# A graph attention layer whose neighbour sums go partly through TensorE: scaled rows summed by transposes, one more column of A, and an earlier flag

## The chip, the cores and the metric

The kernel runs on one core of one Trainium2 chip. The metric is the device time of one execution in microseconds. A core has TensorE (PE; its weight loads are shown as PEld), VectorE (DVE), ScalarE (ACT), GpSimd (POOL) and SyncE (SP), each of which works through its own instructions in a fixed order, and 16 DMA engines that the queues share.

## The reference

There are 3327 nodes with 1024 features; `adj` is symmetric with the diagonal set, about 17 neighbours a row. `bf`, `bg` and `bW` are zero in the data, but the kernel handles them as they come.

```python
h = jnp.maximum(_layernorm(x, axis=-1), 0.0)
f = h @ Wf + bf
g = h @ Wg + bg
e = jax.nn.relu(f @ g.T)
scores = jnp.where(adj > 0, e, NEG)
attention = jax.nn.softmax(scores, axis=1)
x_W = h @ W + bW
return x + attention @ x_W
```

## The kernel before, in words

The scores are needed only where there is an edge, so the kernel (`edge_path`) gathers neighbours. It uses f . g = h (Wf Wg^T) h'^T + terms of the biases, and sums the neighbours' h before it multiplies by W.

Phase 1 (to about 300 us) writes the normalised rows h to memory (`hd`) and each row's list of neighbours (`pd`), ranks the rows by degree into 26 tiles of 128 (`perm`; tile 25 has 127 rows), and makes A = Wf Wg^T (`make_A`, L512), the column u = Wf bg (`uT`, L525 to L528), the row v = bf Wg^T and the number c = bf bg (`make_rows`, L530). v and bW are kept as three bf16 parts each (`split3`, L345, a chain of ten small VectorE operations) and added to a product by a matmul with a matrix of ones over three partitions.

Phase 2 goes over the tiles. A tile has a fixed number of neighbour slots, its cap:

```python
CAPS = [37, 25, 23, 22, 21, 21, 20, 20, 19, 19, 18, 18, 17, 17, 17, 16, 16, 15, 15, 15, 14, 14, 13, 13, 12, 11]
```

For a tile s there are these steps.

- `prepare(s)` (L637): gathers the lists (`pi`) and the tile's own rows (`hp`), transposes hp on TensorE (L632) with copies by ACT (L633) into hT, and makes q = hT' A in two blocks of 512 columns (L650, with the bias row L651, copied by ACT in L652). Eight one-column matmuls (L655) make h.u, to which ACT adds c (`ci`, L657). `df` is the degree column, compared with the cap into `bads` (L659, L660).
- `dots`: for each slot POOL gathers 128 rows of h into a buffer G (L621, a pool of 23 buffers), and VectorE multiplies by q and sums over the row, starting at ci (L673, output `junk`, the sum in `sc`).
- `softmax` (L678) over the tile's scores; its last part on VectorE is the reciprocal `rs` (L696) and the scaling by it (L699). Tiles of cap over 20 (0, 1, 2, 3, 4, 5) go in two halves, the second of which rescales.
- `combine` (L710) forms y, the weighted sum of the gathered rows. Slot 0 starts y on ACT (L732). Most slots are added on VectorE (L734, one pass over 128 x 1024 each). Some, in the tile's last half alone, go to TensorE: ACT writes a diagonal matrix of the weights (L723), and eight fp32 matmuls with it, one for each 128 columns, accumulate the slot's rows, transposed, in the PSUM tile `yT_ps` (L727; an fp32 matmul is two instructions in the trace, so 16 a slot). `on_tensor` (L704) says how many: (4 cap - 52) // 5, which is 16, 9, 8, 7, 6, 6, 5, 5, 4, 4, 4, 4, 3, 3, 3, 2, 2, 1, 1, 1 for tiles 0 to 19 and 0 after, 94 in all.
- `project(s)` (L736): gathers the rows of x (`xp`), adds y's own transposition into the same PSUM tile by eight matmuls with the identity (L746), or transposes y as hp if the tile has no slot there; ACT copies (L751); 16 matmuls by W in two halves, with bW (L756, L757), end in `ps_o`, a ring of two.
- `finish(s)` (L760): VectorE adds x (L765), POOL scatters the rows to `out` (L766).

The program issues dots of tile s + 1 among the steps of tile s, and `prepare(s + 2)` behind `project(s)`. The order on each engine is not written out by hand: a scheduler moves instructions by its own estimate, keeping the dependences, and G's 23 buffers decide when a load can start. At the end VectorE takes the maximum over `bads` (L807), a one-by-one matmul brings it to one partition (L811), VectorE casts it to `flag` (L812), and every engine loads it (L823) and branches (L824): above zero a dense path would compute everything again. That path doesn't run with these data.

## Time and profile before

| what | us |
|---|---|
| runs | 1549.21, 1552.29, 1556.26 (median 1552.29) |
| the profiled execution | 1548.85 |
| its span | 1547.1 |
| PE busy | 1282.8 (83%) |
| DVE busy | 1314.7 (85%) |
| ACT busy | 350.9 (23%) |
| POOL busy | 920.8 (60%) |

The span is what the profile covers; the profiled execution's own time is 1.75 us longer. A row of a timeline reads: start, duration, engine, line, operation, output <- inputs, shapes, count, and in brackets the idle time of the engine before it and what ended it. A row of the waits reads: who waited for what, us in total, times, the longest. PEclk is the clock that TensorE was granted, 1 being full speed. A group of PE rows overlaps its neighbours a little, since matmuls are pipelined.

### The profile page before, as it was taken

The numbers are of one execution on the slowest core, as the hardware profiler recorded it, in microseconds if no ns is written. First come the engines' busy times: TensorE is split into PE (matmuls) and PEld (weight loads), VectorE is DVE, ScalarE is ACT, GpSimd is POOL, SyncE is SP. The second block draws the span as 40 slices with busy tenths as digits, with TensorE's granted clock in tenths as the row PEclk, the third lists the DMA queues.
The fourth block names the chain that finished last, engine by engine and source line by source line (L and its number), as shares of the span: only waits on it lengthen the run. The fifth ranks groups of instructions, "written<-read, shape, count | busy, mean of one in ns | idle before, by whom it ended". The sixth has DMA issues, their size and how long they took to land.

```text
span 1547.1 us, 15226 instructions
## 1 busy us (share of the span) xinstructions
PE 1282.8 (83%) x4904; PEld 718.8 (46%) x4904; DVE 1314.7 (85%) x2664; ACT 350.9 (23%) x646; POOL 920.8 (60%) x625
## 2 busy tenths in 40 slices
PE   1259899394799999999999999999999866979922
PEld 1125453242556765575656545555555432434410
DVE  5878878969799999999998989999999998598750
ACT  6666666110211211121111111111111100011100
POOL 7667867166567665646656566667675666344510
PEclk9999899597899999999999989999999877989966
DMA  8788876387688877858866678777786778445510
GB/s 337 278 349 305 315 265 207 96 349 271 208 318 301 277 250 262 309 177 291 299 241 222 234 245 285 260 264 265 259 283 227 242 250 265 149 146 159 118 41 16
DMA packets 124451, 372.67 MB, mean 241 GB/s; under 512 B 41025, under 2 KB 41425, under 8 KB 121033
## 3 DMA queue, kind: packets, MB, share of 16 engines
q0 software_dynamic: 106288, 286.92, 54.9%
q1 hardware_dynamic: 10860, 70.49, 12.5%
q10 hardware_dynamic: 7212, 14.18, 2.5%
q8 instruction: 41, 0.67, 0.2%
q14 instruction: 50, 0.41, 0.1%
HBM read 343.63 MB, written 27.80 MB: 240 GB/s over the span
## 4 chain that ended last, share of the span: by engine, by line
PE 50%; issue 12%; DVE 8%; POOL 5%; DMA 3%; ACT 1%; POOLq 0%; ACTq 0%; DVEq 0%
PE ps_o L756 19%; PE ps_q L650 15%; PE yT_ps L727 8%; DVE y L734 5%; POOL G L621 4%; PE yT_ps L746 2%; PE ps_t L655 2%; DVE junk L673 2%; DMA G<-hd,pi 2%; PE ps_t L632 1%; PE ps_o L757 1%; PE ps_q L651 1%; DMA xp<-in_x_dram,perm 1%; DVE xp L765 0%; ACT hT L633 0%
## 5 line engine op out<-in xcount | busy, mean ns | idle before, releaser
L621 POOL DMA_INDIRECT G<-hd,pi x468 | 599.2, 1280 | 313.9 <-DVE y L734 128.1
L673 DVE CUSTOM_DVE_ANT_0 junk<-G,q,ci 128x1024 bf16<-128x1024 f32 (+1 forms) x468 | 600.1, 1282 | 49.1 <-DMA G<-hd,pi 37.8
L734 DVE SCALAR_TENSOR_TENSOR y<-G,sc,y 128x1024 f32<-128x1024 f32 (+1 forms) x348 | 447.2, 1285 | 14.6 <-ACT y L732 9.4
L650 PE MATMUL ps_q<-A_sb,hT 128*128 128x512 f32 (+1 forms) x832 | 384.1, 612 | 29.3 <-ACT q L652 24.2
L756 PE MATMUL ps_o<-W_sb,yT 128*128 128x512 f32 (+1 forms) x832 | 383.1, 615 | 4.1 <-ACT yT L751 2.9
L650 PEld LDWEIGHTS ps_q<-A_sb,hT 128*128 128x128 f32 (+1 forms) x832 | 156.2, 195 | 210.5 <-issue 177.7
L756 PEld LDWEIGHTS ps_o<-W_sb,yT 128*128 128x128 f32 (+1 forms) x832 | 159.5, 196 | 202.1 <-issue 189.0
L443 POOL TENSOR_TENSOR r<-r,iotaj 128x3327 f32<-128x3327 f32 (+1 forms) x26 | 188.3, 7250 | 74.4 <-ACT r L442 62.9
L727 PE MATMUL yT_ps<-diag,G 128*128 128x128 f32 x1504 | 176.0, 279 | 1.4 <-ACT diag L723 1.4
L727 PEld LDWEIGHTS yT_ps<-diag,G 128*128 128x128 f32 x1504 | 172.9, 195 | 7.0 <-ACT diag L723 3.6
L452 DVE MAX8 cand<-r 128x8 f32<-128x208 f32 (+2 forms) x416 | 134.0, 361 | 36.7 <-POOL r L443 36.6
L521 PE MATMUL ps_A<-WgT,WfT 128*128 128x512 f32 x256 | 120.6, 631 | 2.9 <-ACT WfT L493 2.9
L652 ACT COPY q<-ps_q 128x512 f32<-128x512 f32 (+1 forms) x52 | 29.4, 591 | 295.4 <-PE ps_q L651 203.9
L521 PEld LDWEIGHTS ps_A<-WgT,WfT 128*128 128x128 f32 x256 | 50.8, 202 | 75.1 <-issue 64.8
L633 ACT COPY hT<-ps_t 128x512 f32<-128x512 f32 (+1 forms) x52 | 29.3, 590 | 220.8 <-PE ps_t L632 128.3
L442 ACT ACTIVATE r<-a 128x3327 f32<-128x3327 int32 (+1 forms) x26 | 77.1, 2967 | 7.8 <-issue 7.8
L765 DVE TENSOR_TENSOR xp<-ps_o,xp 128x512 f32<-128x512 f32 (+1 forms) x52 | 35.7, 687 | 43.6 <-PE ps_o L757 43.6
L766 POOL DMA_INDIRECT out_dram<-xp,perm x26 | 37.8, 1452 | 57.3 <-DVE flag L812 28.2
L621 POOL DMA_INDIRECT xp<-in_x_dram,perm x26 | 29.6, 1137 | 69.3 <-DMA out_dram<-xp,perm 64.1
L621 POOL DMA_INDIRECT hp<-hd,perm x26 | 28.3, 1089 | 63.0 <-PE ps_t L632 36.1
L746 PE MATMUL yT_ps<-ident,y 128*128 128x128 f32 x320 | 48.4, 315 | 20.1 <-DVE y L734 20.1
L746 PEld LDWEIGHTS yT_ps<-ident,y 128*128 128x128 f32 x320 | 46.1, 228 | 23.5 <-DVE y L734 21.8
(139 smaller groups left out, 892.6 us busy)
## 6 DMA issues: line engine op xcount, KB each, us to landing
a<-in_adj_dram SPq DMA_DIRECT2D x25, 1663.5 KB, 8.9
xt<-in_x_dram SPq DMA_DIRECT2D x25, 512.0 KB, 4.3
hd<-xt ACTq DMA_DIRECT2D x25, 512.0 KB, 5.9
G<-hd,pi POOLq DMA_INDIRECT x468, 6.0
wr<-in_L_gnn_Wg_dram SPq DMA_DIRECT2D x8, 512.0 KB, 6.1
wr<-in_L_gnn_Wf_dram SPq DMA_DIRECT2D x8, 512.0 KB, 5.0
W_sb<-in_L_gnn_W_dram SPq DMA_DIRECT2D x1, 4096.0 KB, 14.7
a<-in_adj_dram SPq DMA_DIRECT2D x1, 1455.6 KB, 10.4
```

Source lines behind the costliest of these rows:

```text
L442: nc.scalar.activation(r[:n], a[:n], AF.Relu, accum_out=deg[:n, t : t + 1])
L443: nc.gpsimd.tensor_mul(r[:n], r[:n], iotaj[:n])
L452: nc.vector.max(cand[:n, s * 8 : s * 8 + 8], r[:n, s * SW : min(N, (s + 1) * SW)])
L521: nc.tensor.matmul(ps, WfT[:, k, :], WgT[:, k, o * CB : (o + 1) * CB], start=(k == 0), stop=(k == KD - 1))
L621: nc.gpsimd.indirect_dma_start(out=to, out_offset=None, in_=table, in_offset=bass.IndirectOffsetOnAxis(ap=idx, axis=0),)
L650: nc.tensor.matmul(ps[:n], hT[:, k, :n], A_sb[:, k, o * CB : (o + 1) * CB], start=(k == 0), stop=False)
L673: nc.vector.tensor_tensor_reduce(junk[:n], g[:n], e["q"][:n], 1.0, e["ci"][:n], op0=ALU.mult, op1=ALU.add, accum_out=e["sc"][:n, k : k + 1],)
L727: nc.tensor.matmul(e["yT"][:, c, :n], g[:n, c * P : (c + 1) * P], diag[:n, :n], start=(k == pe[0] and c % 4 == 0), stop=False, skip_group_ ...
L734: nc.vector.scalar_tensor_tensor(y, g[:n], p, y, op0=ALU.mult, op1=ALU.add)
L746: nc.tensor.matmul(e["yT"][:, c, :n], e["y"][:n, c * P : (c + 1) * P], ident[:n, :n], start=False, stop=(c % 4 == 3), skip_group_check=True,)
L756: nc.tensor.matmul(ps[:n], yT[:, k, :n], W_sb[:, k, o * CB : (o + 1) * CB], start=(k == 0), stop=False)
L766: ins = nc.gpsimd.indirect_dma_start(out=out[:, :], out_offset=bass.IndirectOffsetOnAxis(ap=perm[:n, s : s + 1], axis=0), in_=e["xp"][:n], ...
```

## The change

**The slots on TensorE.** `on_tensor` gives cap - 13 slots for (4 cap - 52) // 5: 16, 10, 9, 9, 8, 8, 7, 7, 6, 6, 5, 5, 4, 4, 4, 3, 3, 2, 2, 2, 1, 1 for tiles 0 to 21 and 0 after, 122 in all for 94. A slot is now scaled by ACT in place (the whole G, 128 x 1024, after's L728) and then transposed onto `yT_ps` by eight transposes with the identity that accumulate (after's L711, function `sum_transposed`); the diagonal and its pool are gone. y is added by the same function. VectorE's additions of a slot to y fall from 348 to 320.

**h.u as a column of A.** `A_sb` and `v3` get a column 1024 for u and c, and two of zeros, 1026 in all, so that q is made in three blocks of 342. The one-column matmuls and `ci` are gone; the dot starts at column 1024 of q. c goes through a split3 of its own in `make_rows`.

**The flag.** It is computed in `failed()`, called behind `prepare(25)`, which the program issues in tile 23's turn, and loaded there in the program.

```diff
@@ -296,12 +296,15 @@
...
     O = W.shape[1]
     P = 128
     CB = 512
     KD = D // P
+    QB = 342
+    QW = 3 * QB
     NT = (N + P - 1) // P
     OH = O // CB
     SW = -(-N // SEG)
@@ -336,10 +339,10 @@
     nc.gpsimd.memset(bads, 0.0)
 
     perm = const.tile([P, NT], I32, name="perm")
-    A_sb = wts.tile([P, KD, D], FP, name="A_sb")
-    uT = wts.tile([P, KD], FP, name="uT")
-    c_sb = wts.tile([P, 1], FP, name="c_sb")
-    v3 = wts.tile([3, D], BF, name="v3")
+    A_sb = wts.tile([P, KD, QW], FP, name="A_sb")
+    v3 = wts.tile([3, QW], BF, name="v3")
+    nc.gpsimd.memset(A_sb[:, :, D:], 0.0)
+    nc.gpsimd.memset(v3[:, D:], 0.0)
     bW3 = wts.tile([3, O], BF, name="bW3")
 
     def split3(pool, to, of):
@@ -495,13 +498,11 @@
         WgT = c1.tile([P, KD, D], FP, name="WgT")
         bfT = c1.tile([P, KD], FP, name="bfT")
         bgT = c1.tile([P, KD], FP, name="bgT")
-        bgr = c1.tile([P, KD, P], FP, name="bgr")
         bf3 = c1.tile([P, KD, 3], FP, name="bf3")
         bWf = c1.tile([3, O], FP, name="bWf")
         nc.gpsimd.dma_start(bfT, bf.rearrange("(k p) -> p k", p=P))
         nc.gpsimd.dma_start(bgT, bg.rearrange("(k p) -> p k", p=P))
         nc.gpsimd.dma_start(bWf, bass.AP(tensor=bW.tensor, offset=bW.offset, ap=[[0, 3], [1, O]]))
-        nc.vector.tensor_copy(bgr, bgT[:, :, None].to_broadcast([P, KD, P]))
         nc.vector.tensor_copy(bf3, bfT[:, :, None].to_broadcast([P, KD, 3]))
 
         def load_Wg(c):
@@ -525,14 +526,14 @@
             ps = p_u.tile([P, P], FP, name="ps_u")
             for k in range(KD):
                 nc.tensor.matmul(ps[:, 0:1], WfT[:, k, :], bgT[:, k : k + 1], start=(k == 0), stop=(k == KD - 1))
-            nc.scalar.copy(uT[:, c : c + 1], ps[:, 0:1])
+            nc.scalar.copy(A_sb[:, c, D : D + 1], ps[:, 0:1])
 
         def make_rows():
 
             ps = p_u.tile([P, P], FP, name="ps_u")
             for k in range(KD):
-                nc.tensor.matmul(ps[:, 0:1], bgr[:, k, :], bfT[:, k : k + 1], start=(k == 0), stop=(k == KD - 1))
-            nc.scalar.copy(c_sb, ps[:, 0:1])
+                nc.tensor.matmul(ps[:3, 0:1], bf3[:, k, :], bgT[:, k : k + 1], start=(k == 0), stop=(k == KD - 1))
+            split3(c1, v3[:, D : D + 1], ps[:3, 0:1])
             for o in range(OH):
                 ps = p_mm.tile([P, CB], FP, name="ps_A")
                 for k in range(KD):
@@ -605,7 +606,6 @@
     gpool = ctx.enter_context(tc.tile_pool(name="G", bufs=23))
     hpool = ctx.enter_context(tc.tile_pool(name="hp", bufs=2))
     qpool = ctx.enter_context(tc.tile_pool(name="q", bufs=2))
-    dpool = ctx.enter_context(tc.tile_pool(name="diag", bufs=4))
     hTpool = ctx.enter_context(tc.tile_pool(name="hT", bufs=1))
     ypool = ctx.enter_context(tc.tile_pool(name="y", bufs=2))
     yTpool = ctx.enter_context(tc.tile_pool(name="yT", bufs=1))
@@ -643,18 +643,13 @@
         gather(hp[:n], hd[:, :], perm[:n, s : s + 1])
         hT = hTpool.tile([P, KD, P], FP, name="hT")
         transposed2(hT, hp, n)
-        q = e["q"] = qpool.tile([P, D], FP, name="q")
-        for o in range(OH):
+        q = e["q"] = qpool.tile([P, QW], FP, name="q")
+        for o in range(0, QW, QB):
             ps = p_q.tile([P, CB], FP, name="ps_q")
             for k in range(KD):
-                nc.tensor.matmul(ps[:n], hT[:, k, :n], A_sb[:, k, o * CB : (o + 1) * CB], start=(k == 0), stop=False)
-            nc.tensor.matmul(ps[:n], ones3[:, :n], v3[:, o * CB : (o + 1) * CB], start=False, stop=True)
-            nc.scalar.copy(q[:n, o * CB : (o + 1) * CB], ps[:n])
-        ps = p_t.tile([P, 4, P], FP, name="ps_t")
-        for k in range(KD):
-            nc.tensor.matmul(ps[:n, 0, 0:1], hT[:, k, :n], uT[:, k : k + 1], start=(k == 0), stop=(k == KD - 1))
-        ci = e["ci"] = small.tile([P, 1], FP, name="ci")
-        nc.scalar.activation(ci[:n], ps[:n, 0, 0:1], AF.Identity, bias=c_sb[:n])
+                nc.tensor.matmul(ps[:n, :QB], hT[:, k, :n], A_sb[:, k, o : o + QB], start=(k == 0), stop=False)
+            nc.tensor.matmul(ps[:n, :QB], ones3[:, :n], v3[:, o : o + QB], start=False, stop=True)
+            nc.scalar.copy(q[:n, o : o + QB], ps[:n, :QB])
         df = small.tile([P, 1], FP, name="df")
         nc.vector.tensor_copy(df[:n], pi[:n, KM : KM + 1])
         nc.vector.tensor_scalar(bads[:n, s : s + 1], df[:n], float(CAPS[s]), None, op0=ALU.is_gt)
@@ -671,7 +666,7 @@
         gather(g[:n], hd[:, :], e["pi"][:n, k : k + 1])
         junk = jpool.tile([P, D], BF, name="junk")
         nc.vector.tensor_tensor_reduce(
-            junk[:n], g[:n], e["q"][:n], 1.0, e["ci"][:n], op0=ALU.mult, op1=ALU.add,
+            junk[:n], g[:n], e["q"][:n, :D], 1.0, e["q"][:n, D : D + 1], op0=ALU.mult, op1=ALU.add,
             accum_out=e["sc"][:n, k : k + 1],
         )
 
@@ -703,9 +698,20 @@
 
     def on_tensor(s, k0, k1):
 
-        m = min(max(0, (4 * CAPS[s] - 52) // 5), k1 - k0 - 2)
+        m = min(max(0, CAPS[s] - 13), k1 - k0 - 2)
         ks = range(max(k0, 1), k1)
         return [k for i, k in enumerate(ks) if (i + 1) * m // len(ks) > i * m // len(ks)]
+
+    def sum_transposed(e, g, first, last):
+
+        n = e["n"]
+        if first:
+            e["yT"] = p_y.tile([P, KD, P], FP, name="yT_ps")
+        for c in range(KD):
+            nc.tensor.matmul(
+                e["yT"][:, c, :n], g[:n, c * P : (c + 1) * P], ident[:n, :n], is_transpose=True,
+                start=(first and c % 4 == 0), stop=(last and c % 4 == 3), skip_group_check=True,
+            )
 
     def combine(s, k0, k1, last):
         e = st[s]
@@ -713,21 +719,15 @@
         if not k0:
             e["y"] = ypool.tile([P, D], FP, name="y")
         y = e["y"][:n]
-        e["yT"] = None
+        e["first"] = True
         pe = on_tensor(s, k0, k1) if last else []
         for k in range(k0, k1):
             p = e["sc"][:n, k : k + 1]
             g = G[s, k]
             if k in pe:
-                diag = dpool.tile([P, P], FP, name="diag")
-                nc.scalar.activation(diag[:n, :n], ident[:n, :n], AF.Copy, scale=p)
-                if e["yT"] is None:
-                    e["yT"] = p_y.tile([P, KD, P], FP, name="yT_ps")
-                for c in range(KD):
-                    nc.tensor.matmul(
-                        e["yT"][:, c, :n], g[:n, c * P : (c + 1) * P], diag[:n, :n],
-                        start=(k == pe[0] and c % 4 == 0), stop=False, skip_group_check=True,
-                    )
+                nc.scalar.activation(g[:n], g[:n], AF.Copy, scale=p)
+                sum_transposed(e, g, e["first"], False)
+                e["first"] = False
             elif k == 0:
                 nc.scalar.activation(y, g[:n], AF.Copy, scale=p)
             else:
@@ -739,16 +739,9 @@
         e["xp"] = xpool.tile([P, D], FP, name="xp")
         gather(e["xp"][:n], x[:, :], perm[:n, s : s + 1])
         yT = yTpool.tile([P, KD, P], FP, name="yT")
-        if e["yT"] is None:
-            transposed2(yT, e["y"], n)
-        else:
-            for c in range(KD):
-                nc.tensor.matmul(
-                    e["yT"][:, c, :n], e["y"][:n, c * P : (c + 1) * P], ident[:n, :n],
-                    start=False, stop=(c % 4 == 3), skip_group_check=True,
-                )
-            for g in range(0, KD, 4):
-                nc.scalar.copy(yT[:, g : g + 4, :n], e["yT"][:, g : g + 4, :n])
+        sum_transposed(e, e["y"], e["first"], True)
+        for g in range(0, KD, 4):
+            nc.scalar.copy(yT[:, g : g + 4, :n], e["yT"][:, g : g + 4, :n])
         e["o"] = []
         for o in range(OH):
             ps = p_o.tile([P, CB], FP, name="ps_o")
@@ -771,6 +764,17 @@
         )
         tc.declare_no_dep(ins.ins, group="results", reason="other rows")
         tc.add_to_no_dep_group("results", ins.ins)
+
+    def failed():
+
+        worst = small.tile([P, 1], FP, name="bad")
+        nc.vector.tensor_reduce(worst, bads, AX.X, ALU.max)
+        onesf = small.tile([P, 1], FP, name="onesf")
+        nc.vector.memset(onesf, 1.0)
+        ps = p_o.tile([P, CB], FP, name="ps_o")
+        nc.tensor.matmul(ps[0:1, 0:1], worst, onesf, start=True, stop=True)
+        nc.vector.tensor_copy(flag[0:1, 0:1], ps[0:1, 0:1])
+        return nc.values_load(flag[0:1, 0:1], min_val=0, max_val=1 << 20)
 
     units = []
     for s, cap in enumerate(CAPS):
@@ -800,16 +804,10 @@
             project(s)
             if s + 2 < NT:
                 prepare(s + 2)
+            if s + 2 == NT - 1:
+                bad = failed()
     finish(NT - 1)
-
-
-    bad = small.tile([P, 1], FP, name="bad")
-    nc.vector.tensor_reduce(bad, bads, AX.X, ALU.max)
-    onesf = small.tile([P, 1], FP, name="onesf")
-    nc.vector.memset(onesf, 1.0)
-    ps = p_o.tile([P, CB], FP, name="ps_o")
-    nc.tensor.matmul(ps[0:1, 0:1], bad, onesf[:, 0:1], start=True, stop=True)
-    nc.vector.tensor_copy(flag[0:1, 0:1], ps[0:1, 0:1])
+    return bad
 
 
 def tile_adj_preln_gnn_kernel(tc: tile.TileContext, x, adj, Wf, bf, Wg, bg, W, bW, out):
@@ -819,8 +817,7 @@
     nc = tc.nc
     with tc.tile_pool(name="flag", bufs=1) as fpool:
         flag = fpool.tile([1, 1], I32, name="flag")
-        edge_path(tc, x, adj, Wf, bf, Wg, bg, W, bW, out, flag)
-        bad = nc.values_load(flag[0:1, 0:1], min_val=0, max_val=1 << 20)
+        bad = edge_path(tc, x, adj, Wf, bf, Wg, bg, W, bW, out, flag)
         with tc.If(bad > 0):
             dense_path(tc, x, adj, Wf, bf, Wg, bg, W, bW, out)
 
```

How this moves the instructions is shown at three places. On TensorE, in the middle of the program, from one tile's slots to the next, the kernel before has (G the gathered rows, ident the identity; x32 are the matmuls of four slots):

```order
L727 MATMUL yT_ps<-diag,G 128x128 x32
L650 MATMUL ps_q<-A_sb,hT 128x512 x8
L651 LDWEIGHTS ones_78
L651 MATMUL ps_q<-v_91,ones_78 128x512
L650 MATMUL ps_q<-A_sb,hT 128x512 x8
L651 LDWEIGHTS ones_78
L651 MATMUL ps_q<-v_91,ones_78 128x512
L632 MATMUL ps_t<-ident,hp 128x128 x4
L655 MATMUL ps_t<-uT,hT 128x1 x8
L632 MATMUL ps_t<-ident,hp 128x128 x4
L746 MATMUL yT_ps<-ident,y 128x128 x8
L756 MATMUL ps_o<-W_sb,yT 128x512 x8
```

and the changed one, in a tile that has four slots too:

```order
L711 MATMUL yT_ps<-ident,G 128x128 x32
L650 MATMUL ps_q<-A_sb,hT 128x342 x8
L651 LDWEIGHTS ones_78
L651 MATMUL ps_q<-v_89,ones_78 128x342
L650 MATMUL ps_q<-A_sb,hT 128x342 x8
L651 LDWEIGHTS ones_78
L651 MATMUL ps_q<-v_89,ones_78 128x342
L650 MATMUL ps_q<-A_sb,hT 128x342 x8
L651 LDWEIGHTS ones_78
L651 MATMUL ps_q<-v_89,ones_78 128x342
L632 MATMUL ps_t<-ident,hp 128x128 x8
L711 MATMUL yT_ps<-ident,y 128x128 x8
```

The slots stay at the same place, behind the projection of the tile before; the one-column matmuls that stood among hp's transposes are gone, and q has three blocks.

On VectorE, where tile 21's last y's meet tile 22's dots, before (the number behind a name is its buffer; df_8116 and pi_8065 are tile 25's, sc_7609 tile 22's scores, y_7677 tile 21's sum):

```order
L734 SCALAR_TENSOR_TENSOR y_7677<-G_7650,sc_7435,y_7677 128x1024
L659 CAST df_8116<-pi_8065 127x1
L660 TENSOR_SCALAR bads_85<-df_8116 127x1
L807 TENSOR_REDUCE bad_8322<-bads_85 128x1
L673 ISA junk_7667,sc_7609<-G_7665,q_7570,ci_7602 128x1024
L673 ISA sc_7609 128x1
L673 ISA junk_7671,sc_7609<-G_7669,q_7570,ci_7602 128x1024
L673 ISA sc_7609 128x1
```

In the changed kernel the maximum over `bads` stands here, among tile 24's dots (sc_8086, 12 slots) and tile 23's y's (y_8150):

```order
L691 RECIPROCAL rs_8135<-l_8133 128x1
L657 TENSOR_SCALAR mask_8252<-iotak_76,df_8249 127x40
L694 TENSOR_SCALAR sc_7918<-sc_7918,rs_8135 128x13
L668 ISA junk_8148,sc_8086<-G_8146,q_8047 128x1024
L668 ISA sc_8086 128x1
L771 TENSOR_REDUCE bad_8255<-bads_85 128x1
L734 SCALAR_TENSOR_TENSOR y_8150<-G_7974,sc_7918,y_8150 128x1024
L668 ISA junk_8278,sc_8086<-G_8276,q_8047 128x1024
L668 ISA sc_8086 128x1
L734 SCALAR_TENSOR_TENSOR y_8150<-G_7978,sc_7918,y_8150 128x1024
L668 ISA junk_8282,sc_8086<-G_8280,q_8047 128x1024
L668 ISA sc_8086 128x1
```

The compare and the maximum have moved from before tile 22's dots to a place two tiles on, and dots and y's stand in turns there, where before the dots stood in a row.

On POOL, the loads of tile 25 (127 rows) and the rows around them, before:

```order
L621 DMA G_8169<-hd_67,pi_8065 127x1024
L766 DMA out_0_dram<-xp_7861,perm_87 3327x1024
L621 DMA G_8173<-hd_67,pi_8065 127x1024
L621 DMA G_8177<-hd_67,pi_8065 127x1024
L621 DMA xp_8194<-in_x_dram,perm_87 128x1024
L621 DMA G_8229<-hd_67,pi_8065 127x1024
L621 DMA G_8233<-hd_67,pi_8065 127x1024
L621 DMA G_8237<-hd_67,pi_8065 127x1024
L621 DMA G_8241<-hd_67,pi_8065 127x1024
```

and in the changed kernel:

```order
L621 DMA G_8323<-hd_67,pi_8198 127x1024
L621 DMA G_8327<-hd_67,pi_8198 127x1024
L621 DMA G_8331<-hd_67,pi_8198 127x1024
L621 DMA G_8382<-hd_67,pi_8198 127x1024
L621 DMA G_8386<-hd_67,pi_8198 127x1024
L759 DMA out_0_dram<-xp_7996,perm_87 3327x1024
L621 DMA G_8390<-hd_67,pi_8198 127x1024
L621 DMA xp_8348<-in_x_dram,perm_87 128x1024
L621 DMA G_8394<-hd_67,pi_8198 127x1024
```

Five loads now stand ahead of tile 22's output row and one behind it, where one and two stood; the xp load of tile 24 follows in both. The load of the flag, one row on each engine, stands last in both kernels, behind the last output row on POOL and behind the last projection on TensorE.

## The prediction

> **What bounds the kernel now.** I read the busy times by stage first, then the waits of the two fullest engines, then groups, then single rows. The stages are cut at the reciprocal of the softmax (L696), which VectorE ran for tile 1 at 465.3 us and for tile 21 at 1300.0. Columns: stretch, length, busy time of PE, PEld, DVE, ACT and POOL with instruction counts, granted clock, DMA share, GB/s.
>
> ```profile
> 320.20:465.30 145.10, 110.44 (x512) 68.80 (x511) 126.06 (x194) 22.53 (x51) 96.21 (x79) 0.85 0.81 293
> 465.30:1300.00 834.70, 795.11 (x3237) 462.58 (x3236) 785.83 (x1168) 123.36 (x280) 531.38 (x431) 0.95 0.76 258
> 1300.00:1518.40 218.40, 176.25 (x484) 82.41 (x482) 150.12 (x192) 24.07 (x45) 85.70 (x54) 0.88 0.43 132
> ```
>
> I call the second row the bulk. Two engines are nearly full in it: PE idles 834.7 - 795.1 = 39.6 us, DVE 834.7 - 785.8 = 48.9. ACT has 711 us free. So the bulk shrinks only if PE and DVE both lose work. The third row, the tail, leaves DVE idle for 68 of 218 us. The 28.7 us from there to the span's end belong to the last output rows' way to memory. In the bulk DVE waits mostly for the projection's PSUM:
>
> ```profile
> DVE xp L765 <- PE ps_o L757: 22.1, 17, 3.1
> ```
>
> These groups of the bulk carry the terms (count | busy, mean ns | idle before):
>
> ```profile
> L673 DVE CUSTOM_DVE_ANT_0 junk<-G,q,ci 128x1024 bf16<-128x1024 f32 x354 | 453.8, 1282 | 8.6 <-DMA G<-hd,pi 7.3
> L734 DVE SCALAR_TENSOR_TENSOR y<-G,sc,y 128x1024 f32<-128x1024 f32 x258 | 331.6, 1285 | 6.0 <-ACT y L732 3.3 <-ACT y L701 2.4
> L727 PE MATMUL yT_ps<-diag,G 128*128 128x128 f32 x1248 | 147.1, 280 | 0.9 <-ACT diag L723 0.9
> L746 PE MATMUL yT_ps<-ident,y 128*128 128x128 f32 x304 | 46.5, 317 | 20.1 <-DVE y L734 20.1
> L655 PE MATMUL ps_t<-uT,hT 128*128 128x1 f32 x288 | 36.1, 253 | 1.2 <-ACT hT L633 1.2
> L732 ACT ACTIVATE y<-G,sc 128x1024 f32<-128x1024 f32 x19 | 21.8, 1150 | 26.5 <-DVE sc L699 26.4
> ```
>
> One tile of three slots, with PE at work from one projection to the next:
>
> ```profile
> 957.04 7.03 PE L756 MATMUL ps_o<-W_sb,yT 128*128 128x512 f32 x16
> ...
> 971.70 5.62 PE L727 MATMUL yT_ps<-diag,G 128*128 128x128 f32 x48
> ...
> 994.33 1.95 PE L746 MATMUL yT_ps<-ident,y 128*128 128x128 f32 x16
> ...
> 997.01 2.41 PE L756 MATMUL ps_o<-W_sb,yT 128*128 128x512 f32 x5
> ```
>
> From 957.04 to 997.01 are 39.97 us without a gap. PE sets the pace here, and DVE waits for ps_o.
>
> **DVE after.** A dot (junk) and a y take their turns at a fixed step:
>
> ```profile
> 967.83 1.28 DVE L734 SCALAR_TENSOR_TENSOR y<-G,sc,y 128x1024 f32<-128x1024 f32 x1
> 969.03 1.28 DVE L673 CUSTOM_DVE_ANT_0 junk<-G,q,ci 128x1024 bf16<-128x1024 f32 x1
> ...
> 970.23 1.28 DVE L734 SCALAR_TENSOR_TENSOR y<-G,sc,y 128x1024 f32<-128x1024 f32 x1
> ```
>
> That is 2.40 us a pair, 1.20 each; the 1.28 of a row overlaps its neighbour. The new rule gives tiles 1 to 20 105 slots on TensorE where 1248 / 16 = 78 stood. So 27 y's leave DVE: 27 x 1.20 = 32.4, and 785.8 falls to 753.4.
>
> **PE after.** A slot of 16 matmul instructions took 5.62 / 3 = 1.87 us. The new one is 8 transposes with the identity. None accumulates in the trace of before; the nearest rows are hp's transposes, 8 as well, once slow and once fast:
>
> ```profile
> 514.61 1.95 PE L632 MATMUL ps_t<-ident,hp 128*128 128x128 f32 x8
> ...
> 1319.07 1.10 PE L632 MATMUL ps_t<-ident,hp 128*128 128x128 f32 x8
> ```
>
> I take 1.10, since the slots follow directly on the projection's dense matmuls; 1.95, and for a slot priced as today 1.87, are the other end. The bulk's PE: 795.1 - 147.1 + 105 x 1.10 (115.5) - 36.1 (h.u's one-column matmuls, L655) - 23 (y in 8 instructions for 16, half of L746's 46.5) = 704.4. In the tile above, a fourth slot included: 39.97 - 5.62 + 4.40 - 2.0 - 0.9 = 35.9; its 17 dots and, then, 12 y's are 29 x 1.20 = 34.8, and all that DVE does besides is 785.8 - 612 x 1.20 = 51 us in 20 tiles, 2.6 each: 37.4. DVE becomes the bound, by 1.5 us in this tile. The q matmuls are nearly the same columns in three pieces (1026 for 1024) with one more bias row; I charge them nothing, as PE has that much slack, and about 1 us a tile if it has not.
>
> DVE's waits: 22.1 of the 48.9 are for ps_o. In the tile above PE comes 4 us earlier and DVE 1.2, but the add stands between y's at a place that the scheduler fixed, so I halve them: -11. The rest (loads, softmax on ACT) stays. Bulk: 753.4 + 37.9 = 791.3, **-43**. Bounds: all waits gone, 753 (-81); slots at the 1.87 of now, PE 704.4 + 105 x 0.77 = 785 plus a few us idle, some 805 (-30); the half clock is the first rival.
>
> ACT gets 105 x 1.15 = 121 us in the bulk, without even deducting the diagonals: 244 of 791. Behind a chain of up to ten such scalings (11.5 us) wait the copies of q, hT and yT, and PE for them. A slot can be scaled as soon as the softmax is done, while PE is in the 14.3 us of the tile's projection before, which hides the chain; without that cover PE would follow ACT's chain, 1.15 a slot against its own 1.10, and lose little beyond the first scaling: 1.2 us a tile, 23 in all. POOL and DMA: the loads stay; 258 GB/s over 834.7 us become 272 over 791, under the 293 of the first row. Scaled slots free their buffers sooner.
>
> **The tail.** DVE's waits there:
>
> ```profile
> DVE junk L673 <- DMA G<-hd,pi: 14.6, 7, 5.7
> DVE df L659 <- DMA pi<-pd,perm: 13.6, 1, 13.6
> DVE junk L673 <- ACT ci L657: 7.9, 4, 3.6
> DVE y L734 <- ACT y L732: 6.1, 5, 1.2
> ```
>
> The 13.6 is tile 25's degree column, cast ahead of tile 22's dots in the old order. The new one puts cast, maximum and flag behind them and keeps dots and y's in turns to the end; ci is gone. Then tile 25's loads set the end. They have 127 rows for 128, take POOL 2.5 to 3.5 us each and land late, and an xp load (of a ring of two) waits among them for an output row:
>
> ```profile
> 1403.86 1.01 POOL L766 DMA_INDIRECT out_dram<-xp,perm  x1 [0.30 <-DVE y L734]
> 1405.17 2.56 POOL L621 DMA_INDIRECT G<-hd,pi  x1 [0.30 <-DVE y L734]
> 1408.04 3.44 POOL L621 DMA_INDIRECT G<-hd,pi  x1 [0.31 <-DVE y L734]
> 1427.76 1.36 POOL L621 DMA_INDIRECT xp<-in_x_dram,perm  x1 [16.28 <-DMA out_dram<-xp,perm]
> 1429.43 2.60 POOL L621 DMA_INDIRECT G<-hd,pi  x1 [0.31 <-issue]
> ```
>
> ```profile
> G<-hd,pi POOLq DMA_INDIRECT x5, 25.0
> ```
>
> In the new order, from tile 21's reciprocal: 28 dots and 26 y's until the first buffer for tile 25 is free, 65 with 5 for softmaxes and adds, 70; five loads at the mean of the three rows above, 2.87, 14; from the output row's issue to the xp load's, 1427.76 - 1403.86, 24; five more loads, 14; landing, 25; ten y's of tile 25 at 1.28, 13; its last dot, its softmax and what is left of tile 24 before them, an estimate, 8. The last y ends at 168. From there the old end counts:
>
> ```profile
> 1499.30 1.93 PE L632 MATMUL ps_t<-ident,y 127*128 127x127 f32 x8 [28.51 <-DVE y L734]
> ...
> 1518.32 0.14 DVE L812 CAST flag<-ps_o 1x1 int32<-1x1 f32 x1
> 1518.96 2.56 POOL L766 DMA_INDIRECT out_dram<-xp,perm  x1 [28.17 <-DVE flag L812]
> ```
>
> From 1499.2 to 1518.4 are 19, so 187; with the 6.1 of waits for ACT's y, 193, against 218.4: **-25**. Bounds: 0, and -45 where the xp load's wait falls away.
>
> **Flag and head.** The load of the flag still stands last on every engine, behind the last output row, whose landing hides it; the cast that moved is 0.14 us: 0. The flag's matmul takes one of the two ps_o buffers between tile 23's projection and tile 24's; the cast that frees it stands on VectorE right ahead of tile 23's second add, for which tile 24's projection waits anyway. In phase 1 a third split of ten operations of that size runs on VectorE, waiting for TensorE, ahead of the first list of neighbours: +4, three times the bare sum, since each waits for the one before (1.4 to 8). Tile 0 keeps 16 slots and gives back some 2 in PE work. Head: **+2**.
>
> **The sum.** Span 1547.1 - 43 - 25 + 2 = 1481; the profiled execution took 1.75 more than its span and lay 3.4 under the median of the three runs: 1481 + 5.2 = **1486**. A measurement of this kernel tells 0.5% (7.8 us) from no change.
>
> **Rivals.** *First: transposes don't hold the full clock.* Clock drops in the middle of dense work:
>
> ```profile
> 818.40:821.80 3.40, 3.40 (x19) 3.40 (x17) 1.70 (x4) 0.84 (x3) 2.03 (x2) 0.50 0.90 292
> ```
>
> This one follows a burst of one-column matmuls and transposes; which of the two lets it drop, the trace can't say. Slots at 1.95: 704.4 + 105 x 0.85 (89) + y's 17 = 810.6, with 10 us of idle 821: bulk -14, time 1515. The Trainium skill, "TensorE: Matmul & The Clock Gate", Part 4 (PE-mode transpose), says that the full clock does not engage for transposes, which don't count as PE at work in the same way; by that rule the change would give this time, and the trace bears it out only so far that the drops come near transposes. Chance 0.17.
>
> *Second, slower: the half clock outlasts the transposes.* After a cold start the projection's first half took longer:
>
> ```profile
> 1230.43 9.30 PE L756 MATMUL ps_o<-W_sb,yT 128*128 128x512 f32 x16 [0.73 <-ACT yT L751]
> ```
>
> 9.30 against 7.03 in the tile above: 2.27 more. After the slots and after y, in each of 20 tiles: 91. PE 810.6 + 91 + 10 = 911, bulk +77: 1606, slower. It decides from 7.6 us a tile over PE's 704.4 (then the bulk is 31 longer and the time 1560); the half clock alone makes 5.3 of them. With one such drag a tile, 7.6, the time is 1560, which I count as no change. For it: the slots grow to a stretch of 3 to 10 us of nothing but transposes. Against: matmuls at full load stand on both sides. 0.08 for either.
>
> *Third: the tail gives nothing*, because POOL's row of 127-row loads ends no sooner, being set by landings and not by DVE: 1486 + 25 = 1511. For it: the 24 us wait stays in the order. 0.12.
>
> That the flag's part doesn't do what it says is in the forecast. **Chances**: forecast 0.53, first 0.17, third 0.12: faster 0.82. One drag: same 0.08. Two drags, 0.08, and 0.02 for something unseen: slower 0.10. The range holds forecast, first and third, 0.82: down to bulk -81 (1448, taken as 1450), up to the first rival with half the tail's gain gone (1527, taken as 1530).
>
> **What would show it.** Right: 8 transposes of a slot in 1.1 us and a granted clock of 0.95 or more in the bulk; PE busy near 705, DVE near 753 of some 791; DVE's wait for ps_o halved; no wait for tile 25's degrees; last add some 193 us behind tile 21's reciprocal. Wrong: slots at 1.9 and a clock under 0.9 (first), projections of 9 us (second), or PE waiting for the scalings.

## The result, and the profile after

| | before | changed |
|---|---|---|
| median of the runs, us | 1553.47 (1549.21 to 1556.26) | 1507.32 (1502.53 to 1510.19) |
| ratio, with its 95% interval | | 0.9702 (0.9664 to 0.9740) |
| the profiled execution and its span, us | 1548.85, 1547.1 | 1504.68, 1502.9 |
| tile 1's to tile 21's reciprocal (the bulk) | 834.7 | 796.5 |
| from there to the end of the last add (the tail) | 218.4 | 209.0 |
| from there to the span's end | 28.7 | 28.3 |
| start to tile 1's reciprocal (the head) | 465.3 | 469.1 |

The change is faster by 46 us in the median, where 66 were forecast (from the 1552.29 of the first three runs). These are the stages of the changed kernel, in the columns of the first view of the prediction:

```profile
469.10:1265.60 796.50, 737.91 (x2821) 430.63 (x2820) 757.16 (x1140) 211.48 (x320) 507.90 (x432) 0.97 0.78 271
1265.60:1474.50 208.90, 137.01 (x375) 66.60 (x373) 137.95 (x192) 18.87 (x37) 84.59 (x53) 0.82 0.44 136
1474.50:1502.90 28.40, 0.00 (x0) 0.00 (x0) 0.14 (x1) 0.00 (x0) 2.56 (x1) 0.57 0.08 20
```

In the bulk VectorE is now busy in 757 of 796.5 us and TensorE in 738, so VectorE is the fuller of the two; whether it is the bound is tested below. The clock granted to TensorE has risen from 0.95 to 0.97. In the tail VectorE still idles for 71 us. These are its waits, of the bulk (the first two rows) and of the tail (the others):

```profile
DVE xp L758 <- PE ps_o L750: 14.1, 9, 3.4
DVE junk L668 <- DMA G<-hd,pi: 12.5, 12, 2.1
...
DVE junk L668 <- DMA G<-hd,pi: 50.0, 9, 22.2
DVE xp L758 <- PE ps_o L750: 18.9, 3, 8.5
```

The waits for ps_o have fallen from 22.1 to 14.1 in the bulk. In the tail the wait for tile 25's degrees (13.6) is gone, and the waits for neighbours' rows have grown to 50.0. The groups of the bulk that answer to those of before:

```profile
L734 DVE SCALAR_TENSOR_TENSOR y<-G,sc,y 128x1024 f32<-128x1024 f32 x231 | 297.2, 1287 | 1.8 <-ACT y L732 1.1 <-ACT y L696 0.6
L650 PE MATMUL ps_q<-A_sb,hT 128*128 128x342 f32 x955 | 297.2, 460 | 18.6 <-ACT q L652 10.1 <-ACT hT L633 8.2
L728 ACT ACTIVATE G<-G,sc 128x1024 f32<-128x1024 f32 x105 | 111.1, 1137 | 0.0
L711 PE MATMUL yT_ps<-ident,G 128*128 128x128 f32 x840 | 99.5, 275 | 0.0
L711 PE MATMUL yT_ps<-ident,y 128*128 128x128 f32 x160 | 25.7, 313 | 34.4 <-DVE y L734 34.4
```

A slot costs TensorE 99.5 / 105 = 0.95 us, where a diagonal's cost 147.1 / 78 = 1.89. TensorE now waits 34.4 us for the last y of a tile, where it waited 20.1. ACT does 105 scalings of 1.06 us.

### The profile page after: what moved, and what is told of

It reads as the page before. It is cut to its first block, busy times and chain, and to the rows that moved or that the text cites. A ratio compares the mean times of both kernels' runs of the same rounds, so it can differ in the third digit from the quotient of the medians.

```text
span 1502.9 us, 13875 instructions
## 1 busy us (share of the span) xinstructions
PE 1165.0 (78%) x4242; PEld 660.4 (44%) x4242; DVE 1274.7 (85%) x2645; ACT 442.9 (29%) x673; POOL 891.9 (59%) x627
## 4 chain that ended last, share of the span: by engine, by line
DVE 28%; PE 24%; issue 20%; POOL 12%; DMA 11%; ACT 3%; POOLq 0%; ACTq 0%; DVEq 0%
DVE y L734 12%; PE ps_o L749 12%; DMA G<-hd,pi 9%; DVE junk L668 6%; POOL r L446 5%; POOL G L621 5%; PE ps_q L650 5%; PE yT_ps L711 4%; DVE cand L455 3%; PE ps_A L522 2%; DMA pi<-pd,perm 1%; PE ps_A L540 1%; DVE xp L758 1%; ACT r L445 1%; DVE sc L668 1%
## 5 line engine op out<-in xcount | busy, mean ns | idle before, releaser
L668 DVE CUSTOM_DVE_ANT_0 junk<-G,q 128x1024 bf16<-128x1024 f32 (+1 forms) x468 | 601.1, 1284 | 80.7 <-DMA G<-hd,pi 78.1
L650 PE MATMUL ps_q<-A_sb,hT 128*128 128x342 f32 (+1 forms) x1248 | 395.1, 466 | 74.8 <-ACT q L652 64.8
L734 DVE SCALAR_TENSOR_TENSOR y<-G,sc,y 128x1024 f32<-128x1024 f32 (+1 forms) x320 | 411.3, 1285 | 4.8 <-ACT y L732 2.8
L650 PEld LDWEIGHTS ps_q<-A_sb,hT 128*128 128x128 f32 (+1 forms) x1248 | 232.8, 194 | 195.4 <-ACT q L652 67.1
L652 ACT COPY q<-ps_q 128x342 f32<-128x342 f32 (+1 forms) x78 | 32.7, 449 | 342.3 <-DVE sc L668 249.2
L728 ACT ACTIVATE G<-G,sc 128x1024 f32<-128x1024 f32 x122 | 129.0, 1137 | 0.0
L711 PE MATMUL yT_ps<-ident,G 128*128 128x128 f32 x976 | 116.8, 277 | 2.1 <-ACT G L728 2.1
L711 PEld LDWEIGHTS yT_ps<-ident,G 128*128 128x128 f32 x976 | 108.5, 142 | 12.6 <-ACT G L728 5.5
L711 PE MATMUL yT_ps<-ident,y 128*128 128x128 f32 (+1 forms) x208 | 34.4, 320 | 67.4 <-DVE y L734 49.8
L744 ACT COPY yT<-yT_ps 128x512 f32<-128x512 f32 (+1 forms) x52 | 27.8, 586 | 198.2 <-PE yT_ps L711 198.0
L758 DVE TENSOR_TENSOR xp<-ps_o,xp 128x512 f32<-128x512 f32 (+1 forms) x52 | 35.7, 686 | 34.5 <-PE ps_o L750 34.4
L711 PEld LDWEIGHTS yT_ps<-ident,y 128*128 128x128 f32 (+1 forms) x208 | 28.7, 166 | 72.5 <-DVE y L734 37.3
```

The costliest lines, as they stand in the source:

```text
L650: nc.tensor.matmul(ps[:n, :QB], hT[:, k, :n], A_sb[:, k, o : o + QB], start=(k == 0), stop=False)
L668: nc.vector.tensor_tensor_reduce(junk[:n], g[:n], e["q"][:n, :D], 1.0, e["q"][:n, D : D + 1], op0=ALU.mult, op1=ALU.add, accum_out=e["sc"] ...
L711: nc.tensor.matmul(e["yT"][:, c, :n], g[:n, c * P : (c + 1) * P], ident[:n, :n], is_transpose=True, start=(first and c % 4 == 0), stop=(la ...
L728: nc.scalar.activation(g[:n], g[:n], AF.Copy, scale=p)
L734: nc.vector.scalar_tensor_tensor(y, g[:n], p, y, op0=ALU.mult, op1=ALU.add)
L758: nc.vector.tensor_add(xo, e["o"][o][:n], xo)
```

## The experiments

There are twelve runs in four sets. The runs of a set were made together, beside the kernel before, on one chip. In the first set and the last the kernel before itself took 1596 and 1581 us, where it took 1547 to 1555 otherwise. So ratios (time over the time before, with a 95% interval) are read inside a set only; what the traces show of the difference comes with the last set.

**The old number of slots.** The changed kernel with one line as it was:

```diff
-        m = min(max(0, CAPS[s] - 13), k1 - k0 - 2)
+        m = min(max(0, (4 * CAPS[s] - 52) // 5), k1 - k0 - 2)
```

> The changed kernel with the old number of slots on TensorE (94, each scaled by ACT and transposed). Theory: VectorE is the bound after the change (757 of the bulk's 796.5 us), so each y that comes back costs 1.20 us: 28 of them 34, time about 1541. Rival: the gain is TensorE's relief (h.u gone, cheap slots), and TensorE still sets the pace through PSUM waits; then fewer slots cost nothing: about 1505.

It took 1575.97 us beside 1596.3, ratio 0.9887 (0.9846 to 0.9929). Beside the 0.9702 of the changed kernel that is 0.0185 more, near the theory's 0.022, but the two were not run in one set, so this run alone decides nothing.

**More slots on diagonals.** The kernel before with `CAPS[s] - 13` in the same line.

> The kernel before with the new number of slots (122), each still a diagonal and 16 matmul instructions. Theory: TensorE is the bound in the bulk of before, and 27 more slots of 1.87 us are 50 us for it, of which its 40 us of idle time take some 20: about 1583. Rival: VectorE is the bound already, and 27 y's fewer give 32 us: about 1521.

It took 1608.73 us beside 1596.3, ratio 1.0105 (1.0002 to 1.0207). The bulk took 895.1 us, against 865.5 in the flag-only run of the same set, whose bulk has the instructions of before: 30 us more, as the theory has it, with TensorE busy in 865.8 of the 895.1. Some 9 of the 30 may be late copies of the kind described with the last set. A tail of 199.9 instead of 218.4 gave most of it back. So moving y's off VectorE by way of diagonals won nothing, and if anything it lost: in this set TensorE was the bound, not VectorE.

**h.u as a column of A alone.** The kernel before with the second part of the change and no other:

```diff
-            nc.scalar.copy(uT[:, c : c + 1], ps[:, 0:1])
+            nc.scalar.copy(A_sb[:, c, D : D + 1], ps[:, 0:1])
...
-        for o in range(OH):
+        for o in range(0, QW, QB):
...
-            junk[:n], g[:n], e["q"][:n], 1.0, e["ci"][:n], op0=ALU.mult, op1=ALU.add,
+            junk[:n], g[:n], e["q"][:n, :D], 1.0, e["q"][:n, D : D + 1], op0=ALU.mult, op1=ALU.add,
```

> The kernel before with h.u as one more column of A alone. Theory: TensorE loses 2.0 us a tile and pays 0.35 for the third block, 30 us in the bulk, but VectorE stands right behind with 786 of 835 us, so half of the 22 us that it waits for ps_o go, and the third split3 costs 4: about 1545. Rival: TensorE alone is the bound, all 30 come back: about 1525.

It took 1557.35 us beside 1596.3, ratio 0.9764 (0.9692 to 0.9835). These are the bulks of the flag-only run and of this one:

```profile
475.20:1340.70 865.50, 811.67 (x3242) 472.62 (x3241) 786.75 (x1168) 124.62 (x283) 529.23 (x431) 0.94 0.73 249
```

```profile
480.10:1313.20 833.10, 770.34 (x3286) 481.03 (x3285) 788.01 (x1170) 123.49 (x284) 528.98 (x433) 0.96 0.76 259
```

The bulk fell by 32 us with VectorE's work unchanged, which is about the whole of the 30 that TensorE was to save (its busy time fell by 41), as the rival has it. So TensorE set the pace in that set. Whether h.u's column gives as much where the kernel before takes 1547 us, no run shows.

**The flag alone.** The kernel before with `failed()` behind `prepare(25)`.

> The kernel before with the flag computed behind prepare(25) alone. Theory: the 13.6 us that VectorE waits for tile 25's degrees ahead of tile 22's dots go from the tail, but loads of 127 rows then set the end: 5 to 14 us less, about 1543. Rival: the old order of the tail comes from elsewhere and nothing changes: 1553.

It took 1592.2 us beside 1596.3, ratio 0.9985 (0.9944 to 1.0025): no gain that is clear of the noise, as the rival has it. The wait for tile 25's degrees is still in its tail:

```profile
DVE df L659 <- DMA pi<-pd,perm: 13.8, 1, 13.8
```

**Tile 25 loaded over 128 rows.** This begins the second set: the changed kernel with the last tile computed over 128 rows (the spare one is node 0's and is neither compared with the cap nor written out):

```diff
     def prepare(s):
-        n = rows(s)
+        n = P
...
     def finish(s):
         e = st[s]
-        n = e["n"]
+        n = rows(s)
...
```

> The changed kernel with tile 25's loads (lists, own rows, neighbours, x) over 128 rows instead of 127; the spare row loads node 0 and is not written out. Theory: a load of 127 rows lands 25 us after its issue and holds up what stands behind it, and this is where the tail's 50 us of VectorE's waits for G come from (13.1 ahead of tile 22's dot, 22.2 and some 15 ahead of tile 25's): 35 to 45 less, about 1467. Rival: those loads come late because buffers come free late, and the number of rows is nothing: 1500 to 1507.

It took 1459.36 us beside 1547.38, ratio 0.9426 (0.9379 to 0.9474), 46 us under the run with the flag at the end in the same set (below), which has the changed kernel's ratio and tail. The tail fell from 209.0 to 159.0, and VectorE waits there for no neighbour's row at all:

```profile
DVE xp L758 <- PE ps_o L750: 20.3, 4, 8.5
DVE y L734 <- ACT y L732: 1.7, 2, 1.2
```

How long loads take to land, in the changed kernel between 1266 and 1302 us (the first fence), and in this run between 1330 and 1400 us, tile 25's among them (the second):

```profile
G<-hd,pi POOLq DMA_INDIRECT x7, 25.1
hp<-hd,perm POOLq DMA_INDIRECT x1, 27.8
```

```profile
G<-hd,pi POOLq DMA_INDIRECT x13, 5.7
```

**And the last output in two pieces.** As before, and the scatter in 112 and 15 rows, the latter with indices copied to a tile of their own:

```diff
-        ins = nc.gpsimd.indirect_dma_start(
+        for b, m in pieces(s):
+            ins = nc.gpsimd.indirect_dma_start(
...
```

> As the run with 128-row loads, and the last tile's output in two pieces of 112 and 15 rows. Theory: the last scatter's 28 us are again those of 127 rows; 112 land in some 6, 15 in some 5: 18 to 20 less than without the split, about 1448. Rival: the end is the scatter's fixed cost whatever its rows: no less, about 1467.

It took 1437.57 us beside 1547.38, ratio 0.9295 (0.9239 to 0.9351), 22 us less. From the last add to the span's end are 12.4 us, where there were 32.7 without the split. The last scatter's way, without the split and with it:

```profile
out_dram<-xp,perm POOLq DMA_INDIRECT x1, 25.4
```

```profile
out_dram<-xp,perm POOLq DMA_INDIRECT x1, 3.8
out_dram<-xp,rest_rows POOLq DMA_INDIRECT x1, 3.4
```

**More slots still.** The same with `CAPS[s] - 12`.

> As the split one, with one slot more on TensorE in each tile (cap - 12). Theory: VectorE is the bound and TensorE has 58 us to spare in the bulk: some 23 y's less, 27 us less, TensorE 22 more: about 1425. Rival: TensorE or ACT's chain takes over, no change or slower: 1448 and up.

It took 1405.69 us beside 1547.38, ratio 0.9089 (0.9039 to 0.9139), the fastest version of all, 32 us under the split one of the same set. 18 y's have gone rather than 23, since a tile's last half caps the number; 15 of them stood in the bulk. The bulk of the split run and of this one:

```profile
468.70:1262.50 793.80, 736.11 (x2816) 429.89 (x2817) 757.38 (x1142) 210.67 (x319) 508.96 (x432) 0.97 0.77 272
```

```profile
467.10:1231.50 764.40, 732.50 (x2915) 432.94 (x2914) 740.99 (x1128) 228.44 (x335) 489.17 (x434) 0.99 0.80 284
```

VectorE's wait for ps_o in the latter:

```profile
DVE xp L761 <- PE ps_o L753: 5.5, 4, 2.9
```

VectorE loses 16.4 us of work and 13 of waits, of which 8.6 are waits for ps_o (14.1 in the split run), and the bulk shrinks by 29.4. TensorE's busy time doesn't grow. Work taken off VectorE came back in full, so VectorE is the bound, as the theory has it; the waits that went with it make the gain larger than the theory's price.

**The flag back at the end.** The changed kernel with `failed()` behind the last `finish`.

> The changed kernel with the flag computed at the end as before. Theory: the degree column of tile 25 is again cast early and VectorE waits for it, 5 to 14 us more, about 1515. Rival: the order of the tail is set by the rest of the change, and the flag is worth nothing: 1507.

It took 1505.71 us beside 1547.38, ratio 0.9723 (0.9668 to 0.9778), with a tail of 209.2 against the changed kernel's 209.0. As the rival has it, the flag is worth nothing that these runs can tell. There is no wait for the degrees in this tail either, and its loads wait as in the changed kernel:

```profile
DVE junk L668 <- DMA G<-hd,pi: 50.0, 10, 24.3
```

**Bursts.** This run, of one execution, is a set of its own: the changed kernel with work added, whose results nothing uses:

```diff
+        if s == 12 or s == 16:
+            ps = p_t.tile([P, 4, P], FP, name="ps_t")
+            for j in range(240):
+                c = j % KD
+                if s == 12:
+                    nc.tensor.transpose(ps[:, j % 4, :], e["y"][:, c * P : (c + 1) * P], ident)
+                else:
+                    nc.tensor.matmul(ps[:, 0, 0:1], yT[:, c, :], ident[:, 0:1], start=True, stop=True)
```

> The changed kernel with 240 further transposes of y behind tile 12's projection and 240 one-column matmuls behind tile 16's; their results are not used. Theory: transposes back to back hold the full clock, 0.109 us each, 26 us in all at a granted clock of 1.0; the one-column matmuls let it fall to one half within some 7 us. Rival, by the rule that transposes do not engage the full clock: the clock falls in the transposes too, and they take 0.22 each, some 45 us in all.

The timeline of the transposes, and then the stretches with the granted clock (third number from the right), one of the transposes and two of the one-column matmuls, which began at 1184.8:

```profile
984.10 25.99 PE L757 MATMUL ps_t<-ident,y 128*128 128x128 f32 x236
```

```profile
984.20:1009.80 25.60, 25.60 (x235) 25.60 (x236) 4.76 (x6) 0.00 (x0) 8.20 (x8) 1.00 0.52 193
...
1190.00:1194.00 4.00, 4.00 (x21) 4.00 (x20) 0.00 (x0) 0.00 (x0) 0.00 (x0) 0.50 0.28 107
...
1200.00:1259.00 59.00, 59.00 (x278) 59.00 (x278) 0.00 (x0) 0.00 (x0) 0.00 (x0) 0.50 0.00 1
```

236 transposes, which followed dense matmuls, ran at 0.110 us each at a clock of 1.00 to the last. The one-column matmuls had lost half the clock 5 us after their start and ran on at 0.50. The theory holds, and the drop that the prediction shows behind a burst of both can be put down to h.u's matmuls, which the change removed. The other traces agree: in the bulk of before, eight of eleven drops to 0.50 come just behind h.u's matmuls, with TensorE at work in over 90% of the 3.5 us ahead; in the changed kernel and in the run with h.u alone, TensorE idled for over 40% of the 3.5 us ahead of every drop.

**The changed kernel, the old number and h.u alone in one set.** This is the last set: three kernels again, unchanged.

> The changed kernel as it is, as the measure for the next two on the same chip. Both theories: 0.970 of the time before.

> The old number of slots again, now beside the changed kernel itself. Theory: VectorE is the bound, and 28 y's of 1.20 us cost 34: 0.022 of the time before more than the changed kernel. Rival: more than that, because the order that the scheduler makes for the old number has waits of its own: 0.025 and up.

> h.u as a column of A alone, again, now beside the changed kernel. Theory: a good part of the change's gain is h.u's: 0.976 to 0.985 of the time before. Rival: the ratio seen first was owed to that chip, where the kernel before ran slower: 0.99 to 1.0.

Beside 1581.52 us, the changed kernel took 1566.17, ratio 0.9888 (0.9838 to 0.9939); the old number 1564.26, 0.9886 (0.9842 to 0.9931); h.u alone 1553.51, 0.9803 (0.9755 to 0.9850). The expectations of the first two miss: the changed kernel reached 0.9888 and not 0.970, and the number of slots made no difference. That of the third holds, and here h.u alone is 13 us faster than the whole change. The bulk of the changed kernel took 853.6 us in this set, against 796.5, with the same instructions. Where the 57 us went shows in one tile, from y's transposes to the projection, in the profile of the result (the first fence) and in this set (the second):

```profile
750.86 1.97 PE L711 MATMUL yT_ps<-ident,y 128*128 128x128 f32 x8 [6.74 <-DVE y L734]
...
752.92 1.07 ACT L744 COPY yT<-yT_ps 128x512 f32<-128x512 f32 x2 [19.20 <-PE yT_ps L711]
...
753.56 9.46 PE L749 MATMUL ps_o<-W_sb,yT 128*128 128x512 f32 x16 [0.73 <-ACT yT L744]
```

```profile
776.70 1.97 PE L711 MATMUL yT_ps<-ident,y 128*128 128x128 f32 x8 [5.31 <-issue]
...
785.74 1.07 ACT L744 COPY yT<-yT_ps 128x512 f32<-128x512 f32 x2 [24.76 <-remote]
...
796.37 0.69 DVE L758 TENSOR_TENSOR xp<-ps_o,xp 128x512 f32<-128x512 f32 x1 [10.51 <-PE ps_o L750]
```

ACT had nothing to do, and still took up its copy 785.74 - 778.67 = 7.1 us after the last transpose, where it took 0.1. The profile puts the release down to another core or an unknown queue. Since it models the ends of matmuls, it can't tell whether ACT itself was late or the transposes' signal to it.

Such delays, counted over the bulk's tiles from the last transpose's start to the copy's, beyond 1 us each, are 40.3 us in this run, 20.4 with the old number of slots, 9.4 with h.u alone, and 0.2 in the profile of the result. In the first set they are 25.6 with the old number, 14.7 with diagonals, 6.3 with h.u alone and 5.8 with the flag alone. VectorE's wait for ps_o is 61.7 here instead of 14.1. So in these two sets something that isn't in the kernel's instructions delays the copies, above all where ACT scales the slots, and takes back what the slots gain. It is not all of the difference, since the flag-only bulk is 31 us longer than that of before.

What it is was not found. It isn't the chip alone: each of two chips had a set with it and a set without. Nor are busy DMA engines enough: they moved 404 GB/s while that copy was late (776.7 to 785.7 us), but 413 GB/s in the run with cap - 12 between 1017 and 1026 us, where the copy came 0.4 us after the last transpose's start. So the first and the last set can't tell what the number of slots is worth; the run with cap - 12 does.

## Why the prediction was right, and where it was off

The forecast was 1486 in a range of 1450 to 1530. The measured 1507 lies in the range, and the change is faster as forecast, but 21 us of the gain didn't come. By the prediction's own steps:

**DVE in the bulk**: 231 y's, as counted; busy 757.2 for 753.4, waits 39.3 for 37.9; 796.5 for 791. Right, and the run with cap - 12 shows that VectorE becomes the bound. How the 38 us that the bulk lost divide between the slots and h.u's column, no run of an undisturbed set shows. An estimate: h.u alone leaves VectorE 788 us of work, which with the changed kernel's 39 of waits would make a bulk of some 827, so about 30 of the 38 would be the slots'.

**TensorE**: a slot cost 0.95 for 1.10, which is 16 us less in all. TensorE's busy time is 738 for 704 all the same, and this term was off. The q matmuls took 35 us more than before: the new order has 955 / 48 = 19.9 tiles' of them in the stretch where before's held 575 / 32 = 18.0 (1.9 tiles of 14.9 us, 28), and three blocks take a little more than two. The projections took 7 more, and q's bias rows 5. It cost nothing here, since TensorE is not the bound any more. Nor did the chain of scalings on ACT set the time: TensorE waited for the copies of q and hT for 18 us, within the 23 that the prediction allowed.

**The first rival** (transposes don't hold the full clock) fell, by the bulk's 0.97 and by the burst. The Trainium skill, "TensorE: Matmul & The Clock Gate", Part 4 (PE-mode transpose), says that the full clock doesn't engage for transposes; no run here bears that out, and the measurement decides: 1.00 over 26 us of nothing else, behind dense matmuls. Whether transposes alone would raise the clock after idle time was not tried.

**The second rival's drag** is there in small, with another cause. Where TensorE has waited for y (6.74 us in the tile shown), y's transposes take 1.97 instead of 1.1, the first 16 instructions of the projection 9.46 instead of 7.03, and the add that needs them waits 3.39 us. In this kernel the clock falls in TensorE's idleness, not in its transposes. Such places make up most of the 14.1 us of waits for ps_o that are left where 11 were forecast. With cap - 12 slots TensorE idles less and they are 5.5.

**h.u's column** entered only as part of TensorE's relief, for which the prediction took off half of the waits for ps_o, 11 us in all. Alone, on a kernel that TensorE bounded, it took 32 us out of the bulk, in the slower conditions of the first set.

**The flag** is worth nothing, as forecast, on either kernel. The prediction reads from the new order that the cast of tile 25's degrees has moved out of the way, and doesn't say which part of the change moved it. It isn't the flag's: with the flag alone the wait stays (13.8), and without it the wait is gone, so the rest of the change moved the cast.

**The tail** is the step that failed: 9 us for 25. It went wrong at "28 dots and 26 y's until the first buffer for tile 25 is free, 65 with 5 for softmaxes and adds, 70". The first load of a neighbour for tile 25 was issued at 1350.0, 84.4 behind tile 21's reciprocal. VectorE's work up to there was the 70 that the prediction counts; the other 14 are waits, which the sum has at nothing. POOL's rows in the changed kernel:

```profile
1266.80 2.87 POOL L621 DMA_INDIRECT hp<-hd,perm  x1 [0.30 <-issue]
...
1277.52 0.93 POOL L621 DMA_INDIRECT G<-hd,pi  x1 [0.30 <-issue]
1301.92 2.63 POOL L621 DMA_INDIRECT pi<-pd,perm  x1 [23.47 <-DMA G<-hd,pi]
...
1366.83 1.77 POOL L759 DMA_INDIRECT out_dram<-xp,perm  x1 [0.30 <-DVE y L734]
1368.90 2.54 POOL L621 DMA_INDIRECT G<-hd,pi  x1 [0.31 <-issue]
1391.04 0.98 POOL L621 DMA_INDIRECT xp<-in_x_dram,perm  x1 [19.60 <-DMA out_dram<-xp,perm]
```

and VectorE's, at the two longest waits:

```profile
1296.03 1.28 DVE L668 CUSTOM_DVE_ANT_0 junk<-G,q 128x1024 bf16<-128x1024 f32 x1 [13.05 <-DMA G<-hd,pi]
...
1419.20 1.28 DVE L668 CUSTOM_DVE_ANT_0 junk<-G,q 127x1024 bf16<-127x1024 f32 x1 [22.23 <-DMA G<-hd,pi]
```

The load at 1266.80 is tile 25's own rows, the first of 127. The changed order has it ahead of the loads of tile 22's last five neighbours and tile 23's first; in the kernel before it was issued 56 us behind tile 21's reciprocal, not 1. It lands 27.8 us later, those behind it in some 25, and VectorE waits 13.05 for the first of them. So the wait for the degrees was not removed but replaced, by one of the same size. The prediction asked what else of tile 25 sets the end, and counted its neighbours, but the load of its own rows is not in the sum. The rest of the sum held: five loads in 16.8 for 14, 24.2 from the output row to the xp load for 24, five more loads in 13.1 for 14, 49.5 for 46 from the last load's issue (1404.1) to the last y's end (1453.7), and 21 for 25 from there to the last add. The third rival, that the tail gives nothing because landings set it, was nearer to what happened (1511) than the forecast. The longest wait, 22.23 us for the later loads of tile 25, was in the forecast's chain all along.

The 128-row run shows the cause itself: without a load of 127 rows, the tail's 50 us of waits for neighbours vanish. Head: +3.8 for +2. The end: 28.3 for 28.7. The median lay 2.6 above the profiled execution for the 3.4 assumed.

## What to carry to other kernels

When two engines are nearly full, take work from both at once, and price the step on the engine that was the bound: here the same move of y's to TensorE won nothing (it was 0 to 2% slower) at 1.89 us a slot and was part of a 3% gain at 0.95. In the order of a changed kernel look for slow transfers of any kind ahead of those that a full engine waits for, not only for those that the change is about. A tile that is one row short of the others is worth a look at how its transfers land before anything else: here it cost 68 us (1505.7 less 1437.6, in one set), more than the whole change gained.

## What the runs showed of the hardware

An indirect load or store of 127 rows of 4 KB took 25 to 28 us to land, one of 128 rows 5.7 where none of 127 was ahead, and the pieces of 112 and 15 rows 3.8 and 3.4. (The list of neighbours, 127 short rows of 164 bytes, landed in 5.5.) POOL took 2.5 to 3.5 us to issue a load of 127 rows and mostly 0.9 to 2.0 for 128. In the last 9 us of the 27.8 us load the DMA engines' mean busy share was 0.06, one engine of 16, at 25 GB/s. The Trainium skill, "DMA: Bandwidth & Descriptors", in "Why a DMA increments its semaphore by 16 and not by 1", says that a transfer goes to the largest number of engines, up to 16, that divides its slowest dimension, so that 127 partitions go to one (it names an exception for some direct copies). The trace agrees for indirect loads and stores (the share of 0.06 at 127 rows; 112 is 7 times 16).

Transposes accumulated into PSUM at 0.95 us a slot of eight in the bulk. 236 of them in a row held the full clock that they started with, over 26 us; matmuls of one column lost half of it within 5 us.

An idle ACT took up its copy of transposed rows up to 7 us late in two of the four sets, in stretches in which the DMA engines were full; in other sets it was not late beside DMA engines as full. It stays open what held it.
